# The last graph layer: two heads in TensorE's two column halves, and sums of weights taken on two blocks' sums

## The chip, the cores and the metric

The kernel runs on one core of a Trainium2 chip. The metric is the device time of one execution in microseconds (us); lower is better. Engines are named as the profile names them: PE is TensorE's matrix product and PEld its weight load, DVE is VectorE, ACT is ScalarE, POOL is GpSimd, SP is SyncE (here it only issues DMAs). SBUF is the on-chip working memory, PSUM the small memory that TensorE accumulates into, in eight banks of 512 fp32 columns on 128 partitions.

## The reference

The program is a network of four layers over a graph of 3125 nodes with 256 features and 100000 edges. Each layer adds to the features `x` a graph operation, a linear-attention mix and, after it, a routed feed-forward part. The change lies in the graph operation of the last layer, an attention over edges:

```
xp    = (x @ W).reshape(n, 4, 64)                 # four heads of 64
a_src = einsum('nhc,hc->nh', xp, att_src)
a_dst = einsum('nhc,hc->nh', xp, att_dst)
e     = leaky_relu(a_src[src] + a_dst[dst], 0.2)  # one number per edge and head
e_exp = exp(e - segment_max(e, dst)[dst])
denom = segment_sum(e_exp, dst)
out   = segment_sum(e_exp / denom[dst] * xp[src], dst)   # edges and self loops
y     = relu(out)
```

Beside it stands the layer's mix (linear attention with elu features, two layer norms and a two-layer perceptron); both results are added to `x`, and the feed-forward part follows.

## The kernel before, in words

Nodes lie in 25 blocks of 125 (`NB`, `P`). Destination nodes are also cut into 7 pieces (`PIECES`): six of 500 nodes and one of 125. An earlier layer has left in device memory a dense table `ctt_d` of how often each source block is joined to each destination, in bf16. With it the sum over edges becomes a dense product: for a head, a source block and a run of destinations, a tile `z` of 125 sources x up to 1000 destinations holds count x weight, and TensorE multiplies it by the block's features.

`l3_gnn_mix` sets this up. Line 228's products give `xr`, the features of all blocks and heads. In it each head has 65 columns: 64 features and a column of ones, so that the same product also yields the sum of the weights (the denominator) as a 65th row. `us` holds per-source factors, `bias` per-head shifts that cancel in the quotient.

`l3_dense` does the work, in groups. It takes the pieces two at a time (n = 1000 destinations; the last time one piece of 125). For each such pair it first makes `rows` (L1848, L1850), one exponential per destination and head, kept in the space of `xn`. Then it goes over two heads at a time (all four in the small last group). For each of the 25 source blocks it loads the counts `cs` (SP's queue, two DMAs), and per head it does one ACT instruction into `t` (L1869, two buffers), one DVE instruction into `z` (L1872, three buffers) and one product per piece (L1875), which accumulates in `acc` over the 25 blocks: 65 rows, up to 500 columns, one bank each, four banks in all, each with a single buffer. Those four and the four rotating banks of `bank()` fill PSUM. A product of fp32 data is two passes on TensorE, each with a weight load, so the trace has two records for each.

After the 25 blocks `evac` copies the four accumulators to `at` (also in `xn`'s space), on DVE and ACT in turn (L141, L143); TensorE turns each block of 125 destinations (L1886) so that destinations stand on partitions; and `finish` divides the 64 features by the 65th column and adds the positive part to `x`, with five small DVE instructions per block and two heads (L1830 to L1837). `few` marks denominators that are too small; a program-wide flag `viol` made of such marks sends the execution to a general path, which the given data does not take.

At the end of a pair `arrive` is called for its pieces. The mix (`l3_mix_by_pieces`) calls it for its own. When both are in, `follow` of the feed-forward part runs for that piece: layer norm into `row` (one buffer), a copy and the output DMA of `x`, transposes (L2108), gate products (L228), softmax, the ranks within experts (L2129, L2130), and one indirect DMA per block on POOL's queue (L2152).

`together` interleaves `l3_dense` with the mix: both are generators that yield the share of their work that is done, and the one that is behind goes on, where the mix counts as 1.15 times as fast. So the mix ends before the dense work does. Tile, the framework, then gives every engine its own order when the program is built, by its own priorities and dependencies, so that small instructions of one part stand between those of the other; at run time each engine keeps that order.

## Time and profile before

| what | value |
|---|---|
| median of 15 runs | 5078.65 us (5072.98 to 5090.83) |
| the profiled execution's own time | 5080.64 us |
| its span | 5078.9 us |
| mean granted TensorE clock over the span | 0.837 |
| from the first to the last large product of the last graph layer | 3849.4 to 4807.5 us |

The span runs from the first to the last instruction that the profiler recorded. Engine rows give busy time, which for matrix products is the union of overlapping records. In the rows of groups an arrow shows output and inputs, then partitions x elements, the count, busy time, the mean duration, and the idle time of the engine just ahead of these instructions with what ended it. The granted clock is the share of TensorE's full clock that its throttle let through.

### The profile page before, as it was taken

Reading aid. Unit: us, or ns where it says so; the run is one execution under the profiler, and the core shown is the slowest. Engines: PE = TensorE matmul, PEld = TensorE weight load, DVE = VectorE, ACT = ScalarE, POOL = GpSimd, SP = SyncE. Lnnn points to the kernel's source line nnn. Section 1 sums busy time; section 2 is a strip of 40 time slices with the busy share of each in tenths; the row PEclk is TensorE's granted clock in tenths of the full one; section 3 lists DMA queues with packets and bytes.
Section 4 is the critical chain, followed back from the end, with each engine's and each line's share of the span. In section 5 each row is a group of like instructions: output and inputs, shape, how many; then the busy total and the mean of one; then the engine's idle time right before and its main releaser. Section 6 shows DMA issues by size and latency. Waiting matters only on the chain. (4 is left out here: it accounts for less than half of the span.)

```text
span 5078.9 us, 49526 instructions
## 1 busy us (share of the span) xinstructions
PE 3806.3 (75%) x16425; PEld 2490.3 (49%) x16425; DVE 2492.6 (49%) x7836; ACT 1291.3 (25%) x2300; POOL 1125.4 (22%) x1124
## 2 busy tenths in 40 slices
PE   1885985899476899985454555555879999899698
PEld 1674983666244565554343333333554444444365
DVE  6885343454656211133343434445364656657534
ACT  1475100111123132322000000000235644456511
POOL 1000004000441100004766666666000000000011
PEclk8786985899688799997666766777989999999799
DMA  5255411443220000003333333333121111111142
GB/s 174 63 142 128 106 32 53 133 119 118 70 62 25 3 13 13 13 1 87 90 93 92 92 94 91 94 87 88 29 75 48 52 46 43 48 39 52 22 139 71
DMA packets 256290, 360.32 MB, mean 71 GB/s; under 512 B 62959, under 2 KB 199096, under 8 KB 256027
## 3 DMA queue, kind: packets, MB, share of 16 engines
q1 hardware_dynamic: 132514, 168.96, 11.7%
q0 software_dynamic: 66480, 135.56, 10.2%
q10 hardware_dynamic: 57033, 52.54, 4.0%
q8 instruction: 135, 2.21, 0.2%
q14 instruction: 128, 1.05, 0.1%
HBM read 270.31 MB, written 94.92 MB: 72 GB/s over the span
## 5 line engine op out<-in xcount | busy, mean ns | idle before, releaser
L1526 POOL DMA_INDIRECT hg<-hx_d,idx x841 | 829.4, 986 | 1054.5 <-DVE kmx L753 665.9
L1539 PE MATMUL acc<-hg,to 128*125 128x256 f32 x1682 | 573.6, 493 | 554.5 <-DVE to L1537 266.8
L1539 PEld LDWEIGHTS acc<-hg,to 128*125 128x125 f32 x1682 | 387.0, 244 | 727.3 <-DVE to L1537 305.0
L1875 PE MATMUL acc<-z,xr 125*65 125x500 f32 (+1 forms) x1400 | 571.1, 546 | 8.3 <-DVE z L1872 5.0
L1872 DVE SCALAR_TENSOR_TENSOR z<-t,us,cs 125x1000 f32<-125x1000 f32 (+1 forms) x400 | 410.0, 1029 | 176.0 <-PE acc L1875 134.1
L1869 ACT ACTIVATE t<-xn,us 125x1000 f32<-125x1000 f32 (+1 forms) x400 | 409.7, 1038 | 246.3 <-DVE z L1872 242.4
L1875 PEld LDWEIGHTS acc<-z,xr 125*65 125x65 f32 x1400 | 183.4, 139 | 323.1 <-issue 275.8
L1535 DVE TENSOR_SCALAR to<-iota_f,rel_b,wgt 128x125 f32<-128x125 f32 x841 | 269.9, 356 | 101.2 <-remote 72.2
L1537 DVE SCALAR_TENSOR_TENSOR to<-lock,keep,to 128x125 f32<-128x125 f32 x841 | 256.1, 343 | 120.7 <-remote 68.5
L1396 DVE SCALAR_TENSOR_TENSOR x<-ps,lg,x 125x256 f32<-125x256 f32 x200 | 94.0, 483 | 437.0 <-PE ps L228 437.0
L234 PE MATMUL ps<-xt,w 128*128 128x500 f32 (+1 forms) x672 | 271.7, 549 | 1.7 <-issue 1.7
L2152 POOL DMA_INDIRECT bx_d<-row,slot x25 | 32.0, 1282 | 1008.4 <-issue 520.2
L168 ACT ACTIVATE rstd_t<-rstd_t 125x4 f32<-125x4 f32 (+2 forms) x86 | 17.4, 205 | 828.1 <-DVE rstd_t L167 651.1
L566 PE MATMUL ps<-y,cb 125*125 125x256 bf16 x1875 | 221.6, 283 | 0.0
L774 ACT ACTIVATE k<-k 125x128 f32<-125x128 f32 x50 | 15.8, 316 | 807.2 <-DVE k L773 286.0
L566 PEld LDWEIGHTS <-cb 125*125 125x125 bf16 x1875 | 218.2, 143 | 0.2
L216 PE MATMUL ps<-ident,xn 125*128 125x125 f32 x300 | 64.3, 359 | 176.1 <-DVE xn L182 170.5
L228 PE MATMUL ps<-wo,h 128*125 128x256 f32 x800 | 187.7, 386 | 3.4 <-ACT h L1390 2.3
L234 PE MATMUL ps<-h,w 128*128 128x500 f32 (+1 forms) x448 | 178.8, 542 | 1.1 <-ACT h L1385 1.1
L234 PEld LDWEIGHTS ps<-xt,w 128*128 128x128 f32 x672 | 123.6, 195 | 112.0 <-issue 106.9
L228 PEld LDWEIGHTS ps<-wo,h 128*125 128x125 f32 x800 | 143.0, 187 | 66.0 <-ACT h L1390 43.8
L234 PE MATMUL pl<-xbt,w 128*128 128x384 f32 x416 | 168.9, 555 | 8.2 <-DVE xbt L1125 5.8
(557 smaller groups left out, 6257.8 us busy)
## 6 DMA issues: line engine op xcount, KB each, us to landing
cs<-ctt_d SPq DMA_DIRECT2D x150, 218.8 KB
w<-in_L_ffn_w_dram SPq DMA_DIRECT2D x52, 512.0 KB
cnt_d<-cd SPq DMA_DIRECT2D x25, 683.6 KB
cb<-cnt_d SPq DMA_DIRECT2D x25, 683.6 KB
ctt_d<-ct ACTq DMA_DIRECT2D x6, 2734.4 KB
hg<-hx_d,idx POOLq DMA_INDIRECT x841
b0x_d<-zero SPq DMA_DIRECT2D x1, 9984.0 KB
xb<-b0x_d SPq DMA_DIRECT2D x26, 384.0 KB
```

Source lines behind the costliest of these rows:

```text
L216: self.nc.tensor.transpose(ps[:, j * P:(j + 1) * P], src[:, i // P + j, h * 128:(h + 1) * 128], self.ident[:P, :P])
L228: self.nc.tensor.matmul(ps, xt[:, h, b * P:(b + 1) * P], w[:, h, :], start=(h == 0), stop=(h == k - 1))
L234: self.nc.tensor.matmul(ps, w[:, h, :], xt[:, h, i:i + n], start=(h == 0), stop=(h == k - 1))
L566: nc.tensor.matmul(ps[:P, :D], cf[k][:, h * P:(h + 1) * P], y3[:, b0 + k, j, :], start=(k == 0 and j == 0), stop=(k == m - 1 and j == 2))
L1396: nc.vector.scalar_tensor_tensor(self.x[:, b, :], ps[:P, :D], g[:, b, e:e + 1], self.x[:, b, :], op0=OP.mult, op1=OP.add)
L1526: nc.gpsimd.indirect_dma_start(out=hg[:, j, :], out_offset=None, in_=hx, in_offset=bass.IndirectOffsetOnAxis(ap=idx[:, c + j:c + j + 1], a ...
L1535: nc.vector.tensor_scalar(to, self.iota_f[:, :P], rel[:, c + j:c + j + 1], wgt[:, c + j:c + j + 1], op0=OP.is_equal, op1=OP.mult)
L1537: nc.vector.scalar_tensor_tensor(to, lock[:, b, :], keep[:, j:j + 1], to, op0=OP.max, op1=OP.mult)
L1539: nc.tensor.matmul(ps, to, hg[:, j, :D], start=(c + j == c0[b]), stop=(c + j == c0[b + 1] - 1))
L1869: nc.scalar.activation(t[:, :n], rows[:, k4, :n], AF.Relu, bias=us[:, 2, b, k4:k4 + 1], scale=us[:, 0, b, k4:k4 + 1])
L1872: nc.vector.scalar_tensor_tensor(z[:, :n], t[:, :n], us[:, 1, b, k4:k4 + 1], c, op0=OP.add, op1=OP.mult)
L1875: nc.tensor.matmul(acc[h, k][:, :w], xr[:, b, k4, :], z[:, k * PW:k * PW + w], start=(b == 0), stop=(b == NB - 1))
```

## The change

Each head's products now use 64 columns of TensorE's array and no column of ones. Of two heads, the first takes the array's columns 0 to 63 and the second columns 64 to 127 (`tile_position`), and they write the upper and lower 64 partitions of one accumulator of 128 rows. A second accumulator per piece takes the sums of the weights: products of a 64-column tile of ones with `z`, whose result holds the sum in all 64 rows of a head. They are made on every second block: DVE first adds the two blocks' `z` tiles (block 24 goes alone), and the earlier tile holds the sum. So `z` has five buffers; `t` moves into the space that `at` had.

`finish` works straight from the two accumulators, for a piece and two heads at once: mark, clamp, reciprocal and product on 128 rows x 500 columns, then four transposes of 128 rows, and one DVE instruction that adds the positive part to `x`. The evacuations to `at` are gone. `arrive` for a pair's pieces is called after block 5 of the first heads of the next pair, and for the last piece at the end.

```
@@ -1770,13 +1770,12 @@
             mix = self.l3_mix_by_pieces(ms, mw)
             next(mix)
             wx = self.attn_cols(sb, w, "wx", ["L3_gnn_att_src", "L3_gnn_att_dst"])
-            xr = sb.tile([P, NB, 4, 65], F32, name="xr")
-            nc.gpsimd.memset(xr[:, :, :, 64:65], 1.0)
+            xr = sb.tile([P, NB, 4, 64], F32, name="xr")
             al = sb.tile([P, NB, 8], F32, name="al")
             for b in range(NB):
                 ps = self.bank()
                 self.mm_tok(ps[:P, :264], self.xt, b, wx)
-                nc.vector.tensor_copy(xr[:, b, :, :64], ps[:P, :D].rearrange("p (h d) -> p h d", h=4))
+                nc.vector.tensor_copy(xr[:, b], ps[:P, :D].rearrange("p (h d) -> p h d", h=4))
                 nc.scalar.copy(al[:, b, :], ps[:P, 256:264])
             m = sb.tile([P, 8], F32, name="m")
             nc.vector.tensor_reduce(m, al.rearrange("p b h -> p h b"), axis=AX.X, op=OP.max)
@@ -1819,25 +1818,32 @@
 
     def l3_dense(self, sb, wk, pa, wx, xr, us, bias):
 
+
+
         nc = self.nc
-        few = sb.tile([P, NB, 4], F32, name="few")
+        pairs = [(h0, p0 + k) for p0 in range(0, len(PIECES), 2) for h0 in (0, 2) for k in range(len(PIECES[p0:p0 + 2]))]
+        few = sb.tile([128, len(pairs)], F32, name="few")
         free = self.xn.rearrange("p b d -> p (b d)")
         rows = free[:, :8 * PW].rearrange("p (h d) -> p h d", h=4)
-        at = free[:65, 8 * PW:12 * PW].rearrange("p (h d) -> p h d", h=2)
-
-        def finish(b, h0, nh, acc):
-
-            nc.vector.tensor_scalar(few[:, b, h0:h0 + nh], acc[:, :, 64], 1e-20, None, op0=OP.is_lt)
-            rd = wk.tile([P, 4], F32, name="rd")
-            nc.vector.tensor_scalar(rd[:, :nh], acc[:, :, 64], 1e-20, None, op0=OP.max)
-            nc.vector.reciprocal(rd[:, :nh], rd[:, :nh])
-            t = wk.tile([P, 4, 64], F32, name="tf")
-            nc.vector.tensor_mul(t[:, :nh], acc[:, :, :64], rd[:, :nh, None].to_broadcast([P, nh, 64]))
-            v = self.x[:, b, h0 * 64:(h0 + nh) * 64]
-            nc.vector.scalar_tensor_tensor(v, t[:, :nh].rearrange("p h d -> p (h d)"), 0.0, v,
+        spare = [free[:, j * PW:(j + 2) * PW] for j in (8, 10)]
+
+        def finish(h0, p, f, d):
+
+            i, w = PIECES[p]
+            at = wk.tile([128, PW], F32, name="at", bufs=1)
+            nc.vector.tensor_scalar(at[:, :w], d, 1e-20, 0.0, op0=OP.is_lt, op1=OP.add,
+                                    accum_out=few[:, pairs.index((h0, p)):pairs.index((h0, p)) + 1])
+            nc.vector.tensor_scalar(at[:, :w], d, 1e-20, None, op0=OP.max)
+            nc.vector.reciprocal(at[:, :w], at[:, :w])
+            nc.vector.tensor_mul(at[:, :w], f, at[:, :w])
+            ps = self.bank()
+            for j in range(w // P):
+                nc.tensor.transpose(ps[:P, j * 128:(j + 1) * 128], at[:, j * P:(j + 1) * P], self.ident)
+            v = self.x[:, i // P:(i + w) // P, h0 * 64:h0 * 64 + 128]
+            nc.vector.scalar_tensor_tensor(v, ps[:P, :w // P * 128].rearrange("p (b d) -> p b d", d=128), 0.0, v,
                                            op0=OP.max, op1=OP.add)
 
-        done = 0
+        done, there = 0, []
         for p0 in range(0, len(PIECES), 2):
             pcs = PIECES[p0:p0 + 2]
             n = sum(w for _, w in pcs)
@@ -1849,12 +1855,10 @@
                                          self.xt[:, c, i:i + w], start=(c == 0), stop=(c == HB - 1))
                     nc.scalar.activation(rows[:, h, k * PW:k * PW + w], ps[:P, :w], AF.Exp, bias=bias[:, h:h + 1],
                                          scale=0.8)
-            hg = 4 if n < PW else 2
-            for h0 in range(0, 4, hg):
-                acc = {}
-                for h in range(hg):
-                    for k in range(len(pcs)):
-                        acc[h, k] = pa.tile([65, 512], F32, name=f"acc{h * len(pcs) + k}")
+            for hs in ((0, 2),) if n < PW else ((0,), (2,)):
+                acc = {(h0, k, v): pa.tile([128, 512], F32, name=f"acc{(j * len(pcs) + k) * 2 + v}")
+                       for j, h0 in enumerate(hs) for k in range(len(pcs)) for v in range(2)}
+                old = {}
                 for b in range(NB):
                     cs = wk.tile([P, 2, PW], BF, name="cs", bufs=3)
                     if len(pcs) == 2:
@@ -1863,41 +1867,48 @@
                     else:
                         self.move(nc.sync, cs[:, 0, :n], self.ctt_d[p0, :, b, :n])
                         c = cs[:, 0, :n]
-                    for h in range(hg):
-                        k4 = h0 + h
-                        t = wk.tile([P, 2 * PW], F32, name="t5")
-                        nc.scalar.activation(t[:, :n], rows[:, k4, :n], AF.Relu, bias=us[:, 2, b, k4:k4 + 1],
-                                             scale=us[:, 0, b, k4:k4 + 1])
-                        z = wk.tile([P, 2 * PW], F32, name="z", bufs=3)
-                        nc.vector.scalar_tensor_tensor(z[:, :n], t[:, :n], us[:, 1, b, k4:k4 + 1], c,
-                                                       op0=OP.add, op1=OP.mult)
+                    for h0 in hs:
+                        zs = []
+                        for h in (h0, h0 + 1):
+                            t = spare[h % 2]
+                            nc.scalar.activation(t[:, :n], rows[:, h, :n], AF.Relu, bias=us[:, 2, b, h:h + 1],
+                                                 scale=us[:, 0, b, h:h + 1])
+                            z = wk.tile([P, 2 * PW], F32, name="z", bufs=5)
+                            nc.vector.scalar_tensor_tensor(z[:, :n], t[:, :n], us[:, 1, b, h:h + 1], c,
+                                                           op0=OP.add, op1=OP.mult)
+                            zs.append(z)
                         for k, (i, w) in enumerate(pcs):
-                            nc.tensor.matmul(acc[h, k][:, :w], xr[:, b, k4, :], z[:, k * PW:k * PW + w],
-                                             start=(b == 0), stop=(b == NB - 1))
-                        done += n
+                            for j, z in enumerate(zs):
+                                nc.tensor.matmul(acc[h0, k, 0][64 * j:64 * j + 64, :w], xr[:, b, h0 + j, :],
+                                                 z[:, k * PW:k * PW + w], start=(b == 0), stop=(b == NB - 1),
+                                                 tile_position=(0, 64 * j))
+                        if b % 2 == 0 and b < NB - 1:
+                            old[h0] = zs
+                            continue
+                        if b % 2:
+                            for j, z in enumerate(zs):
+                                zs[j] = old[h0][j]
+                                nc.vector.tensor_add(zs[j][:, :n], zs[j][:, :n], z[:, :n])
+                        for k, (i, w) in enumerate(pcs):
+                            for j, z in enumerate(zs):
+                                nc.tensor.matmul(acc[h0, k, 1][64 * j:64 * j + 64, :w], self.ones[:P, :64],
+                                                 z[:, k * PW:k * PW + w], start=(b == 1), stop=(b == NB - 1),
+                                                 tile_position=(0, 64 * j))
+                    done += n * 2 * len(hs)
                     yield done / (NB * N * 4)
-                if hg == 2:
-                    for h in range(2):
-                        for k, (i, w) in enumerate(pcs):
-                            self.evac(at[:, h, k * PW:k * PW + w], acc[h, k][:, :w])
-                    for j in range(n // P):
-                        ps = self.bank()
-                        for h in range(2):
-                            nc.tensor.transpose(ps[:P, h * 65:(h + 1) * 65], at[:, h, j * P:(j + 1) * P],
-                                                self.ident[:65, :65])
-                        finish(p0 * 4 + j, h0, 2, ps[:P, :130].rearrange("p (h c) -> p h c", h=2))
+                    if b == 5:
+                        for i in there:
+                            self.arrive(i)
+                        there = []
+                for h0 in hs:
+                    for k, (i, w) in enumerate(pcs):
+                        finish(h0, p0 + k, acc[h0, k, 0][:, :w], acc[h0, k, 1][:, :w])
                         yield done / (NB * N * 4)
-                else:
-                    for h in range(4):
-                        self.evac(at[:, h // 2, h % 2 * P:(h % 2 + 1) * P], acc[h, 0][:, :P])
-                    ps = self.bank()
-                    for h in range(4):
-                        nc.tensor.transpose(ps[:P, h * 65:(h + 1) * 65], at[:, h // 2, h % 2 * P:(h % 2 + 1) * P],
-                                            self.ident[:65, :65])
-                    finish(p0 * 4, 0, 4, ps[:P, :260].rearrange("p (h c) -> p h c", h=4))
-            for i, w in pcs:
-                self.arrive(i)
-        nc.vector.tensor_reduce(self.viol[:P, 5:6], few.rearrange("p b h -> p (b h)"), axis=AX.X, op=OP.add)
+
+            there = [i for i, w in pcs]
+        for i in there:
+            self.arrive(i)
+        nc.vector.tensor_reduce(self.viol[:, 5:6], few, axis=AX.X, op=OP.add)
 
     def l3_mix_by_pieces(self, sb, wk):
         nc, a = self.nc, self.a
```

## The prediction

> **What bounds the kernel now.** I read the page's totals first, then the span in 40 slices, to find the stage that the change touches; then that stage alone by groups, by waits, and as a timeline. The totals and slices:
>
> ```profile
> PE 3806.3 (75%) x16425; PEld 2490.3 (49%) x16425; DVE 2492.6 (49%) x7836; ACT 1291.3 (25%) x2300; POOL 1125.4 (22%) x1124
> ...
> PE   1885985899476899985454555555879999899698
> ...
> DVE  6885343454656211133343434445364656657534
> ...
> PE 3%; issue 2%; DMA 0%; POOL 0%; DVE 0%; SPq 0%; POOLq 0%; DVEq 0%
> ```
>
> The last layer's graph stage is slices 31 to 38 of 40: PE near 9, DVE 5 to 7. The chain of waits (its last line here) follows only some 5% of the span, so it says nothing of this stage; groups and stretches must. The first large product starts at 3849.4 us and the last accumulator is copied out at 4808; the mix ends at about 4672. Stretches, with columns length, PE, PEld, DVE, ACT, POOL busy, granted clock, DMA:
>
> ```profile
> 3849.00:4808.00 959.00, 881.97 (x2730) 405.56 (x2728) 609.32 (x1293) 519.54 (x651) 30.86 (x24) 0.94 0.17 44
> 3849.00:4672.00 823.00, 777.91 (x2339) 353.17 (x2338) 521.00 (x1029) 439.52 (x510) 21.10 (x16) 0.96 0.17 46
> 4672.00:4808.00 136.00, 104.05 (x392) 52.39 (x390) 88.32 (x266) 80.02 (x141) 9.75 (x8) 0.82 0.14 33
> ```
>
> TensorE is the bound: 882 of 959 us, DVE 609. Inside, by groups (busy, mean ns, idle before and its releaser):
>
> ```profile
> L1875 PE MATMUL acc<-z,xr 125*65 125x500 f32 x1200 | 528.5, 584 | 2.2 <-DVE z L1872 2.2
> L1872 DVE SCALAR_TENSOR_TENSOR z<-t,us,cs 125x1000 f32<-125x1000 f32 x297 | 371.4, 1255 | 155.5 <-PE acc L1875 133.4 <-ACT t L1869 17.4 <-ACT k_r L1240 1.1
> ```
>
> DVE waits 133 us for TensorE to free a `z`; TensorE waits 2 us for DVE. TensorE's own idle time in the stage:
>
> ```profile
> PE ps L2108 <- DVE row L182: 38.8, 5, 10.7
> PE ps L2129 <- DVE hot L2125: 16.3, 5, 3.3
> ```
>
> So 55 of its 77 idle us are the follow-up of pieces at the three ends of piece pairs. The timeline gives a pass's price:
>
> ```profile
> 4204.92 3.52 PE L1875 MATMUL acc<-z,xr 125*65 125x500 f32 x8
> 4205.35 0.14 PEld L1875 LDWEIGHTS acc<-z,xr 125*65 125x65 f32 x1 [0.28 <-issue]
> 4205.77 0.14 PEld L1875 LDWEIGHTS acc<-z,xr 125*65 125x65 f32 x1 [0.28 <-issue]
> ```
>
> Weights load every 0.42 us, under the running product: a 500-column fp32 product is two passes of 0.42. The 128-column products of the mix have the same spacing (0.42 at 4201.57 to 4201.99), so 65 columns cost what 128 cost.
>
> **PE, products.** Removed: 600 large products, 1200 passes x 0.42 = 504 us. Added: 600 of 64 columns and 312 on the sums (13 sums for 25 blocks x 4 heads x 6 pieces): 912. No row shows two products side by side, so the bounds are 0.42 per product (halves overlap fully: 383 us) and 0.84 (one after the other: 766). I take the overlap: the two share neither columns, weights, moving operand nor output partitions, and the row shows the array already loading one set of weights under a running product. Passes run in order, though: A1, A2, B1, B2, so only A2 with B1 and B2 with the next A1 can overlap, and each unbroken stretch of such products ends one pass longer. The built program has 135 stretches of large ones, broken by the mix: 135 x 0.42 = 57 us. It has 288 changes between half-array and whole-array products. From the nearest rows, 0 (65 to 128 columns keeps 0.42) to 0.16 (a record's 0.58 less its 0.42 spacing): 0 to 46 us. A nearer row is a change between narrow modes, 32-column transposes after 8-row products at half clock:
>
> ```profile
> 1688.27 1.05 PE L270 MATMUL ps<-bo,gt 8*125 8x256 f32 x2
> 1689.26 0.99 PE L264 MATMUL ps<-ident,lg 125*8 125x125 f32 x4
> ```
>
> The second of two starts 0.43 later, at 1688.70, and the change comes 0.56 after it: 0.13 extra, 0.07 at full clock, and that at most, since this load also waited for DVE. I take it: 288 x 0.07 = 20 us. PE: -504 + 383 + 57 + 20 = **-44 us** (-64 to +328).
>
> Two rules of the Trainium skill speak against this term. "TensorE: Matmul & The Clock Gate", Part 3, gives 2.38x for three column tiles of 512; at that efficiency two tiles give 1.59x (an estimate), the 383 would be 482 and PE +55 instead of -44. "TensorEngine Tiling (Array Packing)", Key Properties, says that changing the tiling mode drains the engine; the row above allows 0.13 us at half clock. No run here shows the first.
>
> **DVE, sums of blocks.** Added 144 adds of 1000 columns and 48 of 125. Rows:
>
> ```profile
> L1947 DVE TENSOR_TENSOR o<-o,L_mix_g 125x1024 f32<-125x1024 f32 x6 | 7.3, 1216 | 0.0
> L1299 DVE TENSOR_TENSOR o<-ps,r 125x128 f32<-125x128 f32 x50 | 12.1, 284 | 0.6
> L141 DVE COPY xn<-acc 65x500 f32<-65x500 f32 x12 | 8.1, 671 | 10.1 <-PE acc L1875 10.1
> L1833 DVE RECIPROCAL rd<-rd 125x2 f32<-125x2 f32 x48 | 7.5, 157 | 0.0
> L867 DVE RECIPROCAL qm<-qm 125x16 f32<-125x16 f32 x6 | 1.5, 249 | 0.1
> ```
>
> 144 x 1.19 + 48 x 0.28 = 185 us. **DVE, finish.** 14 calls. Four ops on 500 columns at 0.67 (the PSUM copy). The reciprocal grows from 157 ns at 2 to 249 at 16 columns, 6.6 ns a column, so 3.4 us at 500 (lower end 0.67, if wide ones go like a copy). 12 x 6.1 + 2 x 2.1 = 78 us (43 to 78). Removed: DVE's half of the evacuations, 8.7, and the five small operations of the old finish (L1830 to L1837: 7.0, 7.2, 7.7, 14.2, 14.3), together 59. DVE: 609 + 185 + 78 - 59 = **813 us** of the stage. Per large step (one block, two heads): DVE 2 x 1.255 + 0.96 x 1.19 = 3.65, PE 2.55; before 2.5 and 3.36. So in unmixed runs DVE becomes the bound, and slower than PE was.
>
> **Waits.** `arrive` moves from the end of a pair to block 5 of the next, with all it issues: norms, transposes, gate products, copies on ACT, 25 scatters on POOL's queue (same number) and the output DMAs on SP's queue, now behind six more `cs` loads. PE can then run products while DVE goes through the chain, but DVE's queue is in order: a wait in it (16 us for a row's scatter before, by the waits) now stands ahead of `z`. Relief 0 to 55 of the 77 idle us; I take 27. New: the next group's first product waits until `finish` has read `acc` (5.4 us of DVE for the first piece, against a 0.67 copy; the next group's `z` stand behind it), at six ends; three have the row products as cover (L1848, some 13 us), two or three have mix: 12 us (0 to 33). New: PE waits for `z` where no mix is between. A step leaves it 3.65 - 2.55 = 1.1 us idle: 0 if DVE has always run ahead, 165 if in all 150 steps never. The tail has 14.5 large steps (88 products): 16 us. Elsewhere the stretches of 20 products and more hold 168, 28 steps: 30 us; five `z` buffers hold two steps, so I take half, 15. Together 31. The small group's pace was ACT's 0.46 per head and block and becomes DVE's 0.35 + 0.48 x 0.28 = 0.485: 100 x 0.025 = +3.
>
> ACT loses half the evacuations (7.4 us) and its two `t` buffers only change place: nothing, covered by ACT's 440 idle us. The ones column's memset (POOL) and the wider copies into `xr` lie ahead of the stage beside PE's products; if the cover went, 25 copies x under 0.1 us. Transposes: about as many.
>
> **Sum.** Stage: PE busy 882 - 44 = 838; idle 77 - 27 + 31 + 12 = 93; small group 3: 934 us against 959, **-25 us**. The profiled execution took 5080.6 (span 5078.9 and 1.7 around it), 2.0 above the median of 15, 5078.65. 5080.6 - 25 - 2.0 = **5054 us**. Its own range: with drains 0, all the relief and no new waits another 20 + 28 + 43 = 91 us less, about 4965 (the stage 843, just above DVE's 813); on the other side up to no change.
>
> **Rivals.**
> 1. *No overlap: slower.* The halves go one after the other: PE +262 (766 - 504), +20 drains, small group 152 products at 0.43 us (42.6 by 100) = 65 against 46, +19; finish +12, relief -27: +286, **5365 us**. For it: no row of this trace has two products at once. In between, with a share f of the overlap, PE has -504 + 766 - (383 - 57) f + 20 = 282 - 326 f; with -27 + 12 + 3 and no waits on `z` the stage breaks even at f = 0.83, so it decides once less than five sixths of the passes overlap.
> 2. *DVE takes over.* 813 us busy; its waits on others of before (np_st 48, k_e 43, rows and scatters 31, xtp 15, q_e 6: 143) stay: 956, no change, **5076**; if half of the 134 us on `z` buffers stays too, **5143**. It decides once DVE idles more than 959 - 813 = 146 us in the stage; it idled 350 before. Against: those waits were long because PE was late.
> 3. *Weights not hidden.* If a half's weights cannot load while the other half streams, each pair of passes pays 0.138: 912 x 0.138 = +126 on PE, -25 + 126 less the 43 of waits that then go: +58, **5137**.
>
> **Chances.** Overlap with a gain: 0.53. Overlap, within 0.2%: 0.09. DVE takes over, slower: 0.13. Weights not hidden or partial overlap: 0.07. No overlap: 0.18. 0.2% (10 us) is about what the runs (5073 to 5091) tell apart. Leaving out no overlap (0.18) and a tail of 0.02 below, the range is 4965 to 5180; faster 0.53, same 0.09, slower 0.38.
>
> **What would show it.** Right: passes of the two heads starting together, L1882 and L1894 at some 0.21 us of PE per pass; the stage some 934 us; DVE over 800; the PE waits on `z` no longer 2 but tens of us; L2108's idle time halved. The add at 1.19, the wide reciprocal at 3.4. Wrong: weight loads of L1882 still 0.42 apart throughout (rival 1), DVE above 95% in long runs with PE waiting (rival 2), 0.56 spacing (rival 3).

## The result, and the profile after

The changed kernel takes **5138.16 us** (median of 6 runs, 5129.92 to 5144.05). The kernel before takes 5080.4 (median of 31, the later runs included). The ratio is **1.0108** (95% interval 1.0096 to 1.0119): slower, by more than five times what the runs can tell apart. The prediction was 5054 us, faster; the measured time lies within its range, and the sign is wrong.

The profiled execution took 5129.3 us (span 5127.2). Its graph stage, from the first to the last large product, lasts 1010.5 us against 957.9, so +52.6 where -25 was forecast. What lies before and after the stage differs by -8 and +4 us, so the loss is in the stage. The page of the profile, totals and slices, and the end of its chain of waits:

```profile
PE 3858.0 (75%) x17103; PEld 2491.4 (49%) x17103; DVE 2666.7 (52%) x7853; ACT 1292.6 (25%) x2294; POOL 1125.7 (22%) x1123
...
PE   1886985899377899975455555555969988999798
...
DVE  6885343544746311143334444455357777777634
...
PE 3%; issue 1%; DMA 0%; POOL 0%; DVE 0%; SPq 0%; POOLq 0%; DVEq 0%
```

In slices 31 to 38 PE is about as full as before, and DVE has gone from 4 to 7 tenths up to 7 in all but the last. The columns of stretches are length, then busy time of PE, PEld, DVE, ACT and POOL, granted clock, DMA. The stage after, and its tail after the mix:

```profile
3841.50:4852.00 1010.50, 920.74 (x3404) 402.39 (x3403) 781.14 (x1307) 519.95 (x644) 31.77 (x24) 0.95 0.16 42
4726.00:4852.00 126.00, 104.68 (x498) 61.01 (x496) 98.34 (x286) 73.64 (x133) 9.82 (x8) 0.82 0.12 28
```

PE's busy time rose from 882 to 921 where a fall to 838 was forecast, and DVE's from 609 to 781. The groups show the new parts (busy, mean ns, idle before and its releaser; PE's two rows from 3849 us on, DVE's over the whole stage):

```profile
L1882 PE MATMUL acc<-z,xr 125*64 125x500 f32 x1185 | 387.4, 602 | 5.3 <-DVE z L1877 5.1 <-DVE at L1838 0.2
L1894 PE MATMUL acc<-z,ones 125*64 125x500 f32 x623 | 221.2, 591 | 1.5 <-DVE z L1891 1.3
L1877 DVE SCALAR_TENSOR_TENSOR z<-xn,us,cs 125x1000 f32<-125x1000 f32 x297 | 365.8, 1251 | 52.5 <-PE acc L1882 26.8 <-ACT xn L1874 19.5 <-issue 3.9
L1891 DVE TENSOR_TENSOR z<-z 125x1000 f32<-125x1000 f32 x144 | 168.1, 1191 | 22.9 <-PE acc L1882 22.2
L1837 DVE RECIPROCAL at<-at 128x500 f32<-128x500 f32 x12 | 39.3, 3272 | 0.2
```

The large products and the products on sums together cover less time than the separate groups suggest, since they overlap; but L1882 alone takes 0.33 us per pass (387.4 / 1185), not the 0.21 that I expected. DVE waited 156 us before `z` in the profile before, most of it for PE; now it waits 53.

**The halves do run at once.** Weight loads while no `z` is late:

```profile
4709.86 0.14 PEld L1882 LDWEIGHTS acc<-z,xr 125*64 125x64 f32 x2 [0.28 <-issue]
4710.28 0.14 PEld L1882 LDWEIGHTS acc<-z,xr 125*64 125x64 f32 x2 [0.28 <-issue]
4710.70 0.14 PEld L1894 LDWEIGHTS acc<-z,ones 125*64 125x64 f32 x2 [0.28 <-issue]
```

Two loads every 0.42 us, where the kernel before had one. A few microseconds on, most loads come singly, and pairs stand where a new `z` has arrived:

```profile
4719.36 0.19 PEld L1882 LDWEIGHTS acc<-z,xr 125*64 125x64 f32 x2
...
4721.43 0.14 PEld L1882 LDWEIGHTS acc<-z,xr 125*64 125x64 f32 x1 [0.28 <-issue]
4721.91 0.19 PEld L1882 LDWEIGHTS acc<-z,xr 125*64 125x64 f32 x2 [0.35 <-DVE z L1877]
```

One step of two heads (eight loads) lasts 2.55 us here (4719.36 to 4721.91), where pairs every 0.42 would take 1.67. DVE over the same stretch, in the tail without mix:

```profile
4715.84 2.30 DVE L1891 TENSOR_TENSOR z<-z 125x1000 f32<-125x1000 f32 x2
4718.06 4.97 DVE L1877 SCALAR_TENSOR_TENSOR z<-xn,us,cs 125x1000 f32<-125x1000 f32 x4
4722.95 2.30 DVE L1891 TENSOR_TENSOR z<-z 125x1000 f32<-125x1000 f32 x2
```

These rows show no idle time (the records hold one gap of 0.12 us): four `z` and two adds fill DVE for 7.11 us (4715.84 to 4722.95), and that is the pace of two blocks and two heads. In the kernel before, PE set it at 6.72 (2 x 3.36). So in this tail the changed kernel is 6% slower, not faster.

**How much time PE spends on one product alone.** A product that waits for the second head's `z` does not always stop PE: its partner of the first head runs alone in the meantime, and PE counts as busy. The rows above don't show this, so I went through all matmul records of the stage in order of time and noted at each moment how many large products were running (0.16 us left off each record's end, the 0.58 of a record against its 0.42 spacing), and, if one alone, whether the next one started within 0.2 us of the end of its `z`:

| us of the stage | before | after |
|---|---|---|
| one large product alone | 531 | 247 |
| of these, the next waits for its `z` | | 166 |
| of these, the next is mix or other work | | 77 |
| two at once | 4 | 301 |
| mix and other products | 325 | 330 |
| idle | 98 | 133 |
| sum | 958 | 1011 |

Which product counts as "the next one" is a matter of choice when passes follow each other without a pause. A narrower reading of the same records, in which the very record that ends a run of single passes must just have got its `z`, gives 142 us instead of 166, and 94 instead of 77; the time alone, 247, does not depend on it.

### The profile page after: what moved, and what is told of

Same layout as the page of the kernel before. It is cut to its first block, busy times and chain, and to the rows that moved or that the text cites. A ratio compares the mean times of both kernels' runs of the same rounds, so it can differ in the third digit from the quotient of the medians.

```text
span 5127.2 us, 50828 instructions
## 1 busy us (share of the span) xinstructions
PE 3858.0 (75%) x17103; PEld 2491.4 (49%) x17103; DVE 2666.7 (52%) x7853; ACT 1292.6 (25%) x2294; POOL 1125.7 (22%) x1123
## 5 line engine op out<-in xcount | busy, mean ns | idle before, releaser
L1874 ACT ACTIVATE xn<-xn,us 125x1000 f32<-125x1000 f32 (+1 forms) x400 | 406.6, 1038 | 233.7 <-DVE z L1877 225.8
L1882 PE MATMUL acc<-z,xr 125*64 125x500 f32 (+1 forms) x1400 | 437.1, 565 | 12.0 <-DVE z L1877 10.8
L1877 DVE SCALAR_TENSOR_TENSOR z<-xn,us,cs 125x1000 f32<-125x1000 f32 (+1 forms) x400 | 404.0, 1025 | 67.6 <-PE acc L1882 28.8
L1894 PE MATMUL acc<-z,ones 125*64 125x500 f32 (+1 forms) x728 | 243.2, 554 | 1.8 <-DVE z L1891 1.5
L1882 PEld LDWEIGHTS acc<-z,xr 125*64 125x64 f32 x1400 | 132.2, 140 | 225.1 <-issue 150.5
L1891 DVE TENSOR_TENSOR z<-z 125x1000 f32<-125x1000 f32 (+1 forms) x192 | 180.8, 964 | 23.2 <-PE acc L1882 22.2
```

What stands on the lines that cost most here:

```text
L1874: nc.scalar.activation(t[:, :n], rows[:, h, :n], AF.Relu, bias=us[:, 2, b, h:h + 1], scale=us[:, 0, b, h:h + 1])
L1877: nc.vector.scalar_tensor_tensor(z[:, :n], t[:, :n], us[:, 1, b, h:h + 1], c, op0=OP.add, op1=OP.mult)
L1882: nc.tensor.matmul(acc[h0, k, 0][64 * j:64 * j + 64, :w], xr[:, b, h0 + j, :], z[:, k * PW:k * PW + w], start=(b == 0), stop=(b == NB - 1) ...
L1891: nc.vector.tensor_add(zs[j][:, :n], zs[j][:, :n], z[:, :n])
L1894: nc.tensor.matmul(acc[h0, k, 1][64 * j:64 * j + 64, :w], self.ones[:P, :64], z[:, k * PW:k * PW + w], start=(b == 1), stop=(b == NB - 1), ...
```

## The experiments

Ten kernels ran, on three chips. On the first two the kernel before took 5082.9 (for no_add, pool_add, arrive_end and before_arrive5) and 5076.1 us (no_recip, pair_only and quarters). On the third it took 4913.8, at a granted clock of 0.854 to 0.860 over the span where the first showed 0.831 to 0.837; there only ratios and stages are read (pair_no_recip, before_arrive12, even_mix), and a time is turned into the others' by the ratio times 5080.4. The theory under test: DVE, no longer PE, sets the pace, and what it gained in work costs time nearly one for one. The rival: products side by side gain little, because the mix breaks their stretches, and the products on sums eat up what is gained.

### Without the adds

```
                                 zs[j] = old[h0][j]
-                                nc.vector.tensor_add(zs[j][:, :n], zs[j][:, :n], z[:, :n])
```

The products on sums read the earlier block's `z` alone, so every second block is missing from the denominators.

> The changed kernel without the 192 additions of two blocks' z tiles on DVE: the sums' products read the earlier block's z alone (so the sums of weights hold only every second block's). TensorE's products, their number, order and halves, and how long each z tile is held, stay. Theory A, DVE's pace holds z back and lets one half's product run alone (some 247 us of the stage with one product, 297 with two): DVE loses 181 us, the time with one product alone falls below 180 us, and the kernel goes to 5040 to 5080 us. Rival B, the mix's products break the stretches and that alone costs the overlap: the time with one product alone stays above 220 us, and the kernel stays at 5115 to 5140 us.

Measured 5053.62 us, ratio 0.9948 (0.9931 to 0.9965); the stage 924.5:

```profile
3851.00:4775.50 924.50, 854.58 (x3404) 384.33 (x3404) 620.10 (x1115) 516.21 (x644) 29.86 (x24) 0.95 0.17 46
```

PE has the same 3404 product records, and the time falls by 84.5 us against the changed kernel. The stage falls by 86 for adds that occupied DVE for 181 (168.1 and 12.7), so not one for one. The time of one product alone falls from 247 to 147, 67 of it for want of the next `z` (48 by the narrower reading). So the adds are what turned a small gain into a loss. The run doesn't separate DVE's time from the order that an add imposes: it overwrites a tile that PE must have read (DVE stood 22.2 us before adds for that), and PE's sums wait for it. And adds for nothing would still bring only a half per cent: the products on sums cost 58 us of stage (the table at the end of this section).

### The adds on POOL

```
-                                nc.vector.tensor_add(zs[j][:, :n], zs[j][:, :n], z[:, :n])
+                                nc.gpsimd.tensor_add(zs[j][:, :n], zs[j][:, :n], z[:, :n])
```

> The changed kernel with the additions of two blocks' z tiles on POOL, which is idle for all but 32 us of the stage. Per two blocks DVE's work falls from 7.1 to 4.9 us. Theory A (DVE's pace): faster than the changed kernel if POOL adds 1000 columns in under 2.5 us, 5060 to 5100 us; were an addition 3.5 us or more, POOL itself would pace the steps at 7 us for two blocks and the time stays at 5130 or goes above. Rival B (broken stretches): 5115 to 5140 us whatever the addition takes below 3 us.

Measured 5253.01 us, ratio 1.0341 (1.0323 to 1.0358); the stage 1123.0. The groups of this kernel's stage:

```profile
L1891 POOL TENSOR_TENSOR z<-z 125x1000 f32<-125x1000 f32 x144 | 377.4, 2639 | 650.7 <-PE acc L1882 567.1 <-DVE z L1877 56.7 <-DVE sm L241 9.9
L1877 DVE SCALAR_TENSOR_TENSOR z<-xn,us,cs 125x1000 f32<-125x1000 f32 x300 | 494.6, 1668 | 122.6 <-PE acc L1882 39.6 <-ACT xn L1874 28.6 <-POOL z L1891 26.5
```

An add takes POOL 2.64 us. None of the ranges held. That DVE's own `z` grew from 1.25 to 1.67 us in the mean was not foreseen. Of the 300, the 189 that overlap no add take 1.25 us, and the 92 that overlap adds for more than half of their time take 2.58; the 300 cost DVE 125 us more than they would in the changed kernel (300 x 0.417), most of the 168 us of adds that it was rid of. With this and smaller instructions that took longer too, DVE is busy for 793 us of the stage, against 781 in the changed kernel: handing the adds away gives it nothing. PE, besides, stood 90 us before products on sums (L1894) until POOL's add was done, against 1.5 for DVE's. How the 112 us of stage divide between the two was not tested.

### The follow-up back at the end of the pair

```
-            there = [i for i, w in pcs]
-        for i in there:
-            self.arrive(i)
+            for i, w in pcs:
+                self.arrive(i)
```

> The changed kernel with the follow-up of a pair's pieces back at the pair's end, as before the change; all else as changed. If moving the follow-up gave relief on TensorE (L2108 and L2129 waited 55 us before, their counterparts under 1 us after), undoing it costs 30 to 55 us: 5168 to 5195 us. If the follow-up's work on DVE costs the same wherever it stands, because DVE paces the stage, the time stays at 5125 to 5150 us. If its place among the products is what costs the small last group its 24 us more (73.7 against 49.6), it falls to 5110 to 5120 us.

Measured 5151.46 us, ratio 1.0146 (1.0129 to 1.0163); the stage 1023.7, 13 more than in the changed kernel. PE's waits for the follow-up are those of the kernel before again:

```profile
PE ps L2118 <- DVE row L182: 24.3, 5, 10.6
PE ps L2139 <- DVE hot L2135: 16.6, 5, 3.5
```

They hold 41 us, against 6 in the changed kernel (the expectation's "under 1 us" overlooked L2119's 6.1); the move took 35 us of PE's idle time away and gained 13. Giving PE work during DVE's follow-up is worth little in the changed kernel. The time lies between the two sizes that I had written down, near the smaller one.

### The follow-up moved in the kernel before, and nothing else

```
+                    if b == 5:
+                        for i in there:
+                            self.arrive(i)
+                        there = []
...
-            for i, w in pcs:
-                self.arrive(i)
+            there = [i for i, w in pcs]
+        for i in there:
+            self.arrive(i)
```

> The kernel before with only the follow-up of a pair's pieces moved to block 5 of the next pair's first heads. There TensorE is the bound and DVE has 350 idle us in the stage, so theory A expects the 55 us of waits for L182 and L2125 to be filled with products: 5025 to 5050 us. Rival: the follow-up in the middle of a group holds DVE's queue and so z, and TensorE waits there instead: 5070 to 5090 us.

Measured **5026.84 us**, ratio **0.9889** (0.9873 to 0.9906); the stage 898.8. This is faster than both kernels. Its stage and its remaining follow-up wait:

```profile
3860.00:4759.00 899.00, 869.99 (x2729) 400.44 (x2727) 600.97 (x1292) 527.13 (x658) 30.15 (x24) 0.97 0.18 47
```

```profile
PE ps L2113 <- DVE row L182: 5.3, 2, 2.7
```

PE is now busy for 870 of 899 us; L2108's 38.8 us of the kernel before are 5.3 here (the line has moved to 2113), L2129's 16.3 have gone from the list. This is what the theory expected. So the one part of the change that is shown to be worth having by itself is the one that I had priced at -27, and in the kernel before, where PE is the bound, it gives -54.

### The same at block 12

```
-                    if b == 5:
+                    if b == 12:
```

> The kernel before with the follow-up of the last pair put behind block 12 of the next group instead of block 5. Theory A (what counts is that the follow-up no longer stands at the end of a group, where the accumulators are emptied too): within 15 us of the 5027 us that block 5 gave. Rival (the place itself counts, since DVE's queue is blocked by the follow-up's waits while z is needed): more than 15 us away, 5045 us or more.

Ratio 0.9935 (0.9918 to 0.9952), that is 5047 us by the other chips' 5080.4; the stage 922.4 with 62 us of PE idle, 18 more than with block 5. The place does matter, against what I expected: some four tenths of the gain of block 5 are gone (the two were timed on different chips, each against the kernel before on its own; the stages agree with the ratios). Why block 5 is better was not pursued.

### Without the wide reciprocals

```
             nc.vector.tensor_scalar(at[:, :w], d, 1e-20, None, op0=OP.max)
-            nc.vector.reciprocal(at[:, :w], at[:, :w])
             nc.vector.tensor_mul(at[:, :w], f, at[:, :w])
```

Features are multiplied by the denominator instead of divided by it.

> The changed kernel without the 14 reciprocals in the new finish (the features are multiplied by the sums of weights instead of divided): DVE loses 12 x 3.27 + 2 x 0.9 = 41 us, and each finish becomes 3.3 us shorter for TensorE's transposes, which wait 53 us in all for it (L1841 for L1838). Theory A (DVE's pace, one engine waiting in turn for the other): about that sum, 5095 to 5115 us. Rival (the finish lies beside the mix's products and does not set the pace): 5125 to 5140 us.

Measured 5093.5 us, just under the theory's range, ratio 1.0038 (1.0026 to 1.0050), that is 5100 us by 5080.4; the stage 971.2. Fourteen instructions with 41 us of DVE (12 x 3.27 and 2 x 0.94) cost 39 us of stage: almost nothing covers them. Each stands at the end of a group, where PE waits for it (L1841 in the waits below) and the next group's `z` stand behind it on DVE's queue.

### The two halves alone

```
-                       for j, h0 in enumerate(hs) for k in range(len(pcs)) for v in range(2)}
-                old = {}
+                       for j, h0 in enumerate(hs) for k in range(len(pcs)) for v in range(1)}
...
-                        if b % 2 == 0 and b < NB - 1:
-                            old[h0] = zs
-                            continue
...
-                                nc.tensor.matmul(acc[h0, k, 1][64 * j:64 * j + 64, :w], self.ones[:P, :64],
...
-                        finish(h0, p0 + k, acc[h0, k, 0][:, :w], acc[h0, k, 1][:, :w])
+                        finish(h0, p0 + k, acc[h0, k, 0][:, :w], acc[h0, k, 0][:, :w])
```

No adds and no products on sums; `finish` divides the features by themselves.

> The changed kernel without sums of weights: no additions on DVE, no products with ones, and finish divides the features by themselves. It leaves the two heads side by side alone, beside DVE work near that of the kernel before (z 401 us, finish 78). If products side by side are worth what the sum in the prediction gave them, the time on TensorE for this part falls from some 536 us to 252 plus 60 to 90 for broken stretches; against the kernel before with the follow-up moved (5027 us) some 100 to 160 us less: 4865 to 4930 us. If stretches broken by the mix eat the overlap (rival B), the time stays above 4990 us.

Some features are below the threshold, so the marks in `few` fire and the general path runs behind the stage (14922 us); only the stage counts here: 866.5 us, 32 less than with the follow-up moved alone, where I expected 100 to 160 less. Taken off that kernel's 5027 us, this is some 4995, which I had given to the rival of broken stretches (above 4990). A second form takes the reciprocals out as well and sets the mark's threshold so low that it does not fire:

```
-            nc.vector.tensor_scalar(at[:, :w], d, 1e-20, 0.0, op0=OP.is_lt, op1=OP.add,
+            nc.vector.tensor_scalar(at[:, :w], d, -1e30, 0.0, op0=OP.is_lt, op1=OP.add,
...
-            nc.vector.reciprocal(at[:, :w], at[:, :w])
```

> Two heads side by side alone: no ones products, no adds, no wide reciprocal. It leaves out the division (features are multiplied by clamped features), and the mark compares with -1e30, so that no general path follows and the time can be read. Theory A (halves do save TensorE's passes, but DVE's sequence of z, finish and mix now sets the pace, so half the products save only tens of us): the stage was 866 us with the reciprocals, 39 of which should go: stage 815 to 840 us, time 4935 to 4985 us. Rival (the finish's chain, not z, held the pair alone back): without reciprocals the stage falls below 800 us, time below 4930 us. Rival 2 (pairing as such saves nothing beyond the move of the follow-up): 5000 us or more.

Ratio 0.9730 (0.9714 to 0.9747), that is 4943 us; the stage 822.5. Its stretch and its longest waits of PEld on `z` and of DVE on PE:

```profile
3675.00:4498.00 823.00, 751.26 (x2678) 338.93 (x2676) 576.72 (x1103) 515.38 (x644) 29.74 (x24) 0.94 0.20 53
```

```profile
PEld acc L1880 <- DVE z L1875: 66.6, 153, 3.3
...
DVE z L1875 <- PE acc L1880: 43.2, 45, 4.9
```

So halves side by side do gain, 76 us of stage against the follow-up moved alone (822.5 and 898.8; the shorter `finish` is in this too, and the two ran on different chips), where 600 products in pairs could give up to 252 (half of the 504 us of the large ones). By the sweep 190 us are two at once and 189 one alone, 121 of them for want of `z` (98 by the narrower reading), most of the rest before mix. So the breaks by the mix have a share in it, though the smaller one. Even with no adds, DVE (577 of 823 us) and PE wait for each other in turn, and DVE is not full.

### Sums in four quarters, without adds

```
-                        if b % 2 == 0 and b < NB - 1:
...
-                                nc.vector.tensor_add(zs[j][:, :n], zs[j][:, :n], z[:, :n])
...
-                                nc.tensor.matmul(acc[h0, k, 1][64 * j:64 * j + 64, :w], self.ones[:P, :64],
-                                                 z[:, k * PW:k * PW + w], start=(b == 1), stop=(b == NB - 1),
-                                                 tile_position=(0, 64 * j))
+                                q = 32 * (2 * (k + h0 // 2 * (len(hs) - 1)) + j)
+                                nc.tensor.matmul(den[q:q + 32, :w], self.ones[:P, :32],
+                                                 z[:, k * PW:k * PW + w], start=(b == 0), stop=(b == NB - 1),
+                                                 tile_position=(0, q))
```

The sums of two heads and two pieces are four products of 32 columns each, on every block; `finish` copies the accumulators, turns them and divides per block, with small reciprocals as in the kernel before. `z` has four buffers here.

> A version in which the sums of weights cost DVE nothing: products with 32 columns of ones for all of two heads and two pieces in the array's four quarters, one bank, on every block, no additions, z in four buffers; finish copies the accumulators out (ACT and DVE in turn), turns them, and takes reciprocals of 16 numbers per partition. TensorE per large step: 1.68 us for features and, if four quarters run at once, 0.84 for sums, together 2.5, as changed; DVE 2.5 instead of 3.65. Theory A: faster than every kernel so far, 4930 to 4990 us. If quarters run one after another (four times 0.84 = 3.36 us more per step less the 0.84), it is slower than 5300 us. If the mix's breaks set the pace: 5020 to 5060 us.

Measured 5101.47 us, ratio 1.0050 (1.0031 to 1.0068); the stage 981.5. The four do run at once (a row below, in the last section), and DVE's load in the stage is down to 572 us, the lowest of all. It is nevertheless slower than before, and no range that I had given held it. One product alone took 242 us, and PE counts as busy for 975 of the stage's 981.5 us. DVE's longest wait is for the products on sums to free a `z`:

```profile
DVE z L1875 <- PE den L1886: 134.0, 104, 5.0
```

So DVE's total is not the whole story: here DVE stands still until PE has used a `z`, and PE half-filled until the next one comes. How much of this is the buffer that this kernel has less, and how much the products on sums on every block, which use each `z` for longer, was not separated; nor was a kernel with more buffers run.

### The mix over the whole stage

```
-            self.together([self.l3_dense(sb, wk, pa, wx, xr, us, bias), mix], (1.0, 1.15))
+            self.together([self.l3_dense(sb, wk, pa, wx, xr, us, bias), mix], (1.0, 1.0))
```

> The changed kernel with the mix counted as fast as the dense work (1.0 instead of 1.15), so that it reaches over the whole stage and leaves no tail of large products alone. Theory A (DVE is late for z throughout, in the mixed parts too, because its one queue holds adds, mix and finish in a row; the tail is only a small part): the tail's price was some 14 us of waits, so 5118 to 5140 us. Rival (the unmixed tail is where DVE bounds and most of the loss arises): 5115 us or less. If the mix at the end only adds its own chain behind the last products: 5145 us or more.

Ratio 1.0096 (1.0080 to 1.0113), that is 5129 us, not to be told from the changed kernel's 1.0108. The stage is 999.7, and the time alone for want of `z` 129 instead of 166 (102 and 142 by the narrower reading). The tail, where DVE bounds outright, is a small part; most of the loss arises beside the mix.

### The chain of stages

| step | stage, us | difference |
|---|---|---|
| kernel before | 957.9 | |
| follow-up moved | 898.8 | -59 |
| halves side by side, new `finish`, no sums | 866.5 | -32 |
| products on sums, no adds | 924.5 | +58 |
| adds on DVE: the changed kernel | 1010.5 | +86 |

Each step is the difference of two profiled executions. The first and the last were also measured as times: 5080.4 to 5026.8, and 5053.6 to 5138.2.

## Why the prediction was wrong

The terms of the predicted stage against the measured one, in the sweep's terms: products, other PE work, PE's idle time. By that count the kernel before has 535 + 325 + 98. The forecast's 25 less are 934 - 959.

| term | predicted, us | measured, us |
|---|---|---|
| large products and sums, `z` always ready | 494 | 465 |
| mix and others on PE | 325 | 330 |
| waits for `z` | 31 | 113 |
| PE waits for `finish` | 12 | 53 |
| PE waits for the follow-up | 28 | 6 |
| other idle | 43 | 44 |
| stage | 933 | 1011 |

The first predicted row is 535 - 504 + 383 + 57 + 20 + 3. Its measured row is 548 (247 + 301) less half of the 166 us alone for want of `z`, since such a pass would otherwise have run beside its partner; that half, 83, and 30 us of idle time before a late `z` make 113. (By the narrower reading, 142, the two rows would be 477 and 101.)

**The step that failed is "Waits": the 31 us for `z`.** I had put DVE's load at 813 us and even noted that in unmixed runs DVE would be the bound, but then counted its lateness only in the tail (16) and in long unmixed stretches (15), as if beside the mix DVE always ran ahead. It does not. A likely reason, not tested by itself, is that its queue also holds the mix's and the follow-up's instructions, in order. The measured size, 101 to 113, lies inside the 0 to 165 that I gave as its ends; taking 31 was the error. The run without adds shows where it comes from: 85 us go with the adds, though PE's products stay the same. Two waits of PE show it in the profile after:

```profile
PEld acc L1882 <- DVE z L1877: 54.3, 130, 2.9
...
PE ps L1841 <- DVE at L1838: 52.6, 9, 6.8
...
PE acc L1882 <- DVE z L1877: 10.8, 19, 2.6
...
PE ps L2119 <- DVE row L182: 6.1, 2, 3.7
```

The first stands for PE's passes that waited while the partner ran (in the kernel before 40.1, where PE itself had other passes to run); the third is the one that I looked at when I wrote "2 us", and it is only 10.8 here. That row alone hides the loss, because PE stays "busy" on half of its columns.

**The second step that failed is the wait for `finish`: 12 (0 to 33) against 53.** Durations were right: the wide reciprocal 3.27 us (predicted 3.4), the four other operations 0.67 to 0.69 (0.67), in all 6.0 per call against 6.1. The price was not: I let the row products or the mix cover it, and the waits show PE standing before its own transposes (L1841) nine times, up to 6.8 us. Without the reciprocals 39 of their 41 us come off the stage.

**Right:** the overlap (Rivals 1 and 3 fall: two weight loads every 0.42 us, and the reloads stay under the passes); the adds, 1.19 us each (1.191). DVE's 813 came out as 781: neighbouring records overlap (taking away 181 us of adds shortens the busy time by 161), and in the kernel before with only the follow-up moved the stage holds 601 instead of 609. The small group cost 24 us more (73.7 against 49.6 for its hundred ACT instructions), not 3.

**Near by luck:** the 57 us for the ends of stretches and the 20 for changes of mode. The 57 rested on the order A1, A2, B1, B2, but the first passes of both heads start together, and an undisturbed stretch ends with both (last section). The 77 us with one product alone before mix or other work (94 by the narrower reading), half of which are lost, come from heads that are out of step. A change of mode costs 0.14 to 0.19 us where 500-column products meet, not 0.07; at that price 288 changes are some 48 us (an estimate that takes every change for one of these: 144 x 0.14 + 144 x 0.19), not 20.

**Too small:** the relief of the follow-up. PE's waits for it fell from 55 to 6, where I took half; alone it gives 54 us. In the changed kernel it gives only 13 of stage, which fits a DVE that is late there anyway.

**Rival 2 is what happened.** It was to decide once DVE idles more than 146 us in the stage; it idles 229 (1010.5 - 781). Its second price, 5143, assumed that half of the 134 us on `z` buffers stays: DVE waits on PE for a `z` to read or free 28.8 us (L1877) and 22.2 (L1891), 51 in all, and the time is 5138. That the price lies so near is partly luck: it had DVE busy for 813 and idle for 210, where 781 and 229 were measured. What spoke against it, that "those waits were long because PE was late", held only in part: two engines that are each busy for 77% and 91% of a stage, with five `z` buffers between them, wait in turn.

**The two rules of the Trainium skill.** "TensorE: Matmul & The Clock Gate", Part 3, would by its figure for three column tiles have cost PE 482 instead of 383 (an estimate); with `z` ready two products ran every 0.42 us, so the trace shows full overlap for two halves in fp32, and the measurement decides. "TensorEngine Tiling (Array Packing)", Key Properties, has the engine drain at a change of mode: the trace shows a pause of about 0.09 us there and a longer first pass behind it (last section), against the 0.07 taken for all of it.

## What to carry to other kernels

Before halving the work of the busiest engine, add up the work that the change gives to its producer and count the pace of one step for each: if the producer's step is now the longer one, and its queue also carries other parts of the program, do not count on it being late only where nothing else runs; here it was late throughout. "Busy" of an engine with two halves does not show that one half stands empty; count the moments with one product alone. A change made of several parts should be taken apart: here the move of the follow-up alone makes the kernel 1.1% faster, and the rest more than undoes it.

## What the runs showed of the hardware

- **Two fp32 products in two column halves interleave from the first pass.** I had assumed the order A1, A2, B1, B2. In the records the first passes of both heads start 7 ns apart (3852.718 and 3852.725), and the stretch of four products at 3852.72 spans 1.83 us to the next product's start (3854.55), against 3.36 for four products one after the other. The rows of PE's timeline:

```profile
3852.72 1.90 PE L1882 MATMUL acc<-z,xr 125*64 125x500 f32 x8
3854.55 1.12 PE L228 MATMUL ps<-wkv,xt 128*125 128x512 f32 x2
```

- **Four quarters too.** In the kernel with 32-column products eight passes start within half a microsecond of 4600.18 (the first four 7 ns apart), and the next product starts at 4601.15, 0.97 us after the first:

```profile
4600.18 1.05 PE L1886 MATMUL den<-z,ones 125*32 125x500 f32 x8
4601.15 1.06 PE L1880 MATMUL acc<-z,xr 125*64 125x500 f32 x4
```

- **A change between whole and half array** costs 0.14 to 0.19 us. Each way the next product starts 0.51 to 0.52 instead of 0.42 us after the last pass starts. The first pass of halves then takes 0.47 (as it does after a wait for `z`), the first of the whole array 0.53 with 500 or 512 columns; in the kernel before, where no product has a `tile_position`, these are 0.42 or 0.43.
- **An fp32 reciprocal costs by its width:** 128 x 500 takes 3272 ns, 128 x 125 takes 940, where a copy of 500 columns takes 671.
- **POOL's adds slow DVE:** the same DVE instruction into `z` takes 1.25 us where it overlaps none of POOL's adds and 2.58 in the mean where it lies beside them for more than half of its time, up to 3.36. The adds themselves take 2.30 us where no `z` instruction overlaps and 2.73 where one does for more than half.
  The Trainium skill, "GPSIMD Engine Reference", section "1. Specifications", says that POOL's access to SBUF is shared with DVE and contended when a DVE instruction has two inputs in SBUF. The instruction into `z` has two large ones, and the durations agree with it. My expectation for that kernel left it out.
